# Attention scores of two heads at a time: float32r parts in the two halves of the array's rows

## The chip, the core and the metric

One NeuronCore of a Trainium2 chip runs the whole program. The metric is the device time of one execution in microseconds; 4454.7 us is the median of three runs before the change (4446.53 to 4455.5).

## What is computed

A batch of 16 sequences of 512 tokens with 256 channels passes through four attention blocks, each behind a layer norm and with a residual. All have 16 heads of 16 channels. Cut to the core:

```python
x = x + attn_a(layernorm(x))     # causal, biases on q, k, v and the output
x = x + ffn(layernorm(x))        # tokens split in two groups by a similarity with g_info
x = x + attn_b(layernorm(x))     # rotary q and k, no mask
x = x + ffn(layernorm(x))

def ffn(x):                      # REG = 5 register tokens in front
    sim = mean over heads of cos(q, g); rescaled to 0..1
    pos = sim > 0.9
    # a token attends to the registers and to the tokens of its own group;
    # a register token takes the mean of its results over both groups
```

Everything is float32, and the softmax scores have to be exact to about that.

## The kernel before, in words

**Stages.** `PLAN` names four stages, a, f, b, f, here called stage 0 to 3. A stage goes through 16 batches, a batch through 4 quads of heads (`NG`), a quad through 4 key tiles of 128 keys (`NT`). So a batch has 16 key tiles.

**Scores in bf16 parts.** A float32 q or k is split into three bf16 parts (`split3`, L329 to L338: one copy on ScalarE, one on VectorE, two subtractions on POOL), and the six products of parts that matter are laid under each other on the contraction rows (`QPARTS`, `KPARTS`): 6 x 16 = 96 rows (`ROWS`). Two rows more carry the group flags of stages f, and two the negated row maximum. The parts go to DRAM (`qd`, `kd`) and come back as two quads of heads at a time (`load_half`, L489 to L510, on the SP queue, three buffers), the flag rows straight from `fd`. One matmul over at most 100 rows gives the scores of one head, 128 x 512.

**Each score is computed twice.** `maxima` (L523) makes the tile s with queries on the partitions (L545) and VectorE takes its maxima (L547; with the causal mask in L552). At the end of a quad `put` (L577 to L588) transposes the maxima on TensorE (mt, L579, in the large score banks), copies them on ScalarE (ms, L581), writes them to DRAM (md, L583) and reads them back into two rows of q (L585); both DMAs are SP's. `products` (L594) then makes the tile t with keys on the partitions (L612), the maximum already subtracted by those rows; in stage a a second matmul adds the causal mask (L620). ScalarE takes exp (L623), and `weigh` (L627, matmul L634) multiplies four heads with the values, side by side in four groups of 32 columns. The sum of a quad is copied to O in L650.

**Fill.** All else is generators: `prep` (layer norm, projections L324 and L415), `tail` (L779: transposes L793 and L813, output projection L833), `registers` (L655) and `masked`. They are drained between scores, after each of the 16 steps of a quad, by cost (`drain`, L874). Their PSUM tiles come from `small` (two banks).

**Order.** The main loop (L919 to L967) emits a t, then advances the maxima, which stay 36 steps ahead (`AHEAD`, four steps per key tile); a `put` follows its last maximum by 8 steps (`WAIT`, L914). The value products of a key tile come one key tile later (`waiting`). Between a and f and between b and f everything is drained and `split` computes the flags. The framework then places each instruction in its engine's queue: in this order, but with others moved ahead where one would wait by its own planning. [...] Fill and scores use different banks: five of 512 columns for s and t, one for the value sums, two for `small`.

Of the kernel before, what the change touches and what calls it, by code (L numbers as in the profile page):

```python
# [40 lines left out]
P = 128  # L42
# [5 lines left out]
RW = 4 * (32 + REG)  # L48
# [6 lines left out]
AHEAD = 36  # L55
WAIT = 8
QPARTS = (0, 1, 2, 0, 1, 0)
KPARTS = (0, 0, 0, 1, 1, 2)
ROWS = 96
# [3 lines left out]
def constants():  # L63
# [7 lines left out]
    c["mask_t"] = np.ascontiguousarray(f(-BIG) * up.T)  # L71
# [4 lines left out]
    c["cos"], c["sin"] = np.repeat(cos, H, axis=0), np.repeat(sin, H, axis=0)  # L76
    c["hm"] = np.concatenate([np.tile(np.eye(H, dtype=f), (8, 1)), np.zeros((P, H), f)], axis=1)
    blk, half = np.zeros((P, H, HV), f), np.zeros((P, REG), f)
    rows = np.zeros((2, 2, RW), f)
    for h in range(H):  # L80
        p, k = 32 * (h // 4), h % 4
        for r in range(REG):
            blk[p + REG * k + r, h] = 1.0
            half[p + REG * k + r, r] = 0.5
            rows[1, :, (32 + REG) * k + r] = 1.0
    c["blk"], c["half"], c["rows"] = blk, half, rows
    clamp = np.full((P, NT, 4), -MASKED, f)
    clamp[P - 1, NT - 1] = 3.0e38
    c["clamp"] = clamp
    reg = np.zeros((P, B, NT), f)  # L90
# [7 lines left out]
def hybrid_kernel(ctx: ExitStack, tc: tile.TileContext, a: dict, out: bass.AP):  # L98
# [3 lines left out]
    def pool(name, bufs, **kw):  # L102
# [10 lines left out]
        pool("pe", 9),  # L113
# [5 lines left out]
    ps_x = pool("ps_x", 5, space=PSUM)  # L119
    ps_o = pool("ps_o", 1, space=PSUM)  # L120
    ps_s = pool("ps_s", 2, space=PSUM)
# [17 lines left out]
    qd = [dram.tile([3, C, S], BF, tag=f"qd{b}", name=f"qd{b}") for b in range(B)]  # L139
    kd = [dram.tile([3, C, S], BF, tag=f"kd{b}", name=f"kd{b}") for b in range(B)]  # L140
    vd = [dram.tile([P, NT, VW], F32, tag=f"vd{b}", name=f"vd{b}") for b in range(B)]
    xd = [dram.tile([P, NT, C], F32, tag=f"xd{b}", name=f"xd{b}") for b in range(B)]
    fd = dram.tile([4, B, S], BF, tag="fd", name="fd")
    md = [dram.tile([NT, 2, 4, P], BF, tag=f"md{i}", name=f"md{i}") for i in range(8)]
# [10 lines left out]
    ident_bf = const.tile([P, P], BF, tag="ident_bf", name="ident_bf")  # L155
    nc.vector.tensor_copy(ident_bf, ident)
# [5 lines left out]
    def load_weights(layer, project):  # L162
# [7 lines left out]
        for i in ws:  # L170
            raw = ptmp.tile([P, 2, C], F32, tag="tmp", name=f"wraw{layer}_{i}")
            nc.sync.dma_start(raw, a[f"{kind}_w"][:, :, i, :])
            if i == WQ:
                nc.vector.tensor_scalar(raw, raw, SCALE, None, ALU.mult)
            k = 0 if project else i
            nc.scalar.copy(wh[:, :, k, :], raw)
            nc.vector.tensor_tensor(wl[:, :, k, :], raw, wh[:, :, k, :], ALU.subtract)
# [9 lines left out]
    bqk = load_const("bqk", [P, 2, 2])  # L187
# [6 lines left out]
    NB = 3  # L194
    Qs, Ks = [], []
    for i in range(NB):
        q = res.tile([P, 8, S], BF, tag=f"qs{i}", name=f"qs{i}")
        k = res.tile([P, 8, S], BF, tag=f"ks{i}", name=f"ks{i}")
        Qs.append(q)
        Ks.append(k)  # L200
# [6 lines left out]
    for i in range(2):  # L207
        t = res.tile([ROWS + 2, 2, RW], BF, tag=f"rst{i}", name=f"rst{i}")
        rst.append(t)
    sim = res.tile([P, B * NT], F32, tag="sim", name="sim")  # L210

    def constant_rows():
        both = ptmp.tile([4, 2, S], BF, tag="tmp", name="zo")
        nc.vector.memset(both[:, 0], 0.0)
        nc.vector.memset(both[:, 1], 1.0)
        for q, k in zip(Qs, Ks):
            for i, t in enumerate((q, k)):
                nc.sync.dma_start(t[ROWS : ROWS + 4], both[:, i].unsqueeze(1).to_broadcast([4, 8, S]))
        for t in rst:
            nc.gpsimd.memset(t, 0.0)  # L220
# [4 lines left out]
    def early_constants():  # L225
        late["mask_s"] = to_bf("mask_s", [P, S])
        late["mask_t"] = to_bf("mask_t", [P, P])
        late["clamp"] = load_const("clamp", [P, NT, 4])
# [4 lines left out]
    def direction():  # L233
# [13 lines left out]
        )  # L247
        ps = small("gt")
        for i in range(2):
            nc.tensor.transpose(ps[:, i * P : (i + 1) * P], g2[:, i * P : (i + 1) * P], ident)  # L250
# [5 lines left out]
    def late_constants():  # L256
# [7 lines left out]
        rows = p1.tile([2, 2, RW], F32, tag="rows", name="rows")  # L264
        nc.sync.dma_start(rows, a["rows"])
        rb = p1.tile([2, 2, RW], BF, tag="rb", name="rb")
        nc.vector.tensor_copy(rb, rows)
        for t in rst:
            nc.sync.dma_start(t[ROWS : ROWS + 2], rb)
# [5 lines left out]
    def prep(layer, b, x):  # L275
# [53 lines left out]
        def split3(which, i, y):  # L329

            t = p4.tile([P, 3, S], BF, tag="parts", name=f"t{which}{n}_{i}")
            nc.scalar.copy(t[:, 0, :], y)  # L332
            sub = nc.vector if which == "k" and layer + b == 0 else nc.gpsimd
            sub.tensor_tensor(y, y, t[:, 0, :], ALU.subtract)  # L334
            nc.vector.tensor_copy(t[:, 1, :], y)  # L335
            sub.tensor_tensor(t[:, 2, :], y, t[:, 1, :], ALU.subtract)  # L336
            d = (qd if which == "q" else kd)[b]
            nc.sync.dma_start(d[:, i * P : (i + 1) * P, :].rearrange("k p q -> p k q"), t)  # L338

        def parts(which, i):  # L340
            ps = small(f"p{which}{n}_{i}")
            yield from project(ps, WQ if which == "q" else WK, i)
            y = ptmp.tile([P, S], F32, tag="tmp", name=f"y{which}{n}_{i}")
            if kind == "a":
                w = 0 if which == "q" else 1
                nc.scalar.activation(y, ps, AF.Identity, bias=bqs[:, w, i : i + 1])
            else:
                nc.scalar.copy(y, ps)
            if kind == "f" and which == "q":
                y2 = ptmp.tile([P, S], F32, tag="tmp", name=f"y2{n}_{i}")  # L350
                nc.scalar.activation(y2, ps, AF.Square)
                st["y", i] = y, y2
            else:
                split3(which, i, y)

        def similar():
# [6 lines left out]
            for i in range(2):  # L363
                split3("q", i, st["y", i][0])
# [14 lines left out]
            else:  # L379
                nc.gpsimd.tensor_tensor(nd[:, 0], nd[:, 0], nhalf, ALU.pow)  # L380
# [4 lines left out]
        def turned(which):  # L385
# [10 lines left out]
            nc.vector.tensor_tensor(b_, y[1], sin, ALU.mult)  # L396
            nc.gpsimd.tensor_tensor(a_, a_, b_, ALU.subtract)
            nc.vector.tensor_tensor(b_, y[0], sin, ALU.mult)
            nc.gpsimd.tensor_tensor(y[1], y[1], cos, ALU.mult)
            nc.gpsimd.tensor_tensor(y[1], y[1], b_, ALU.add)  # L400
            split3(which, 0, a_)
            split3(which, 1, y[1])
# [47 lines left out]
    def split(layer):  # L450
# [22 lines left out]
        fl = p1.tile([P, 4, n], BF, tag="fl", name=f"fl{layer}")  # L473
# [4 lines left out]
        pf = small(f"pf{layer}", BF)  # L478
        for k in range(4):
            nc.tensor.transpose(pf[:n, k * P : (k + 1) * P], fl[:, k, :], ident_bf)  # L480
        fs = p1.tile([n, 4, P], BF, tag="fs", name=f"fs{layer}")
        nc.vector.tensor_copy(fs.rearrange("r k p -> r (k p)"), pf[:n, : 4 * P])
        nc.sync.dma_start(fd.rearrange("k b (t p) -> (b t) k p", p=P), fs)


    halves = [(layer, b, u) for layer in range(len(PLAN)) for b in range(B) for u in range(2)]
    cleared = set()

    def load_half(i):  # L489
        layer, b, u = halves[i]  # L490
        kind = PLAN[layer]
        q, k = Qs[i % NB], Ks[i % NB]
        hs = slice(8 * u, 8 * (u + 1))
        if kind == "b" and i % NB not in cleared:
            cleared.add(i % NB)
            nc.gpsimd.memset(q[ROWS : ROWS + 2].bitcast(F32), 0.0)
        for dst, src, blocks in ((q, qd[b], QPARTS), (k, kd[b], KPARTS)):
            src = src.rearrange("k (d h) s -> (k d) h s", h=H)
            r = 0
            while r < 6:  # L500
                e = r + 1
                while e < 6 and blocks[e] == blocks[e - 1] + 1:
                    e += 1
                p0 = D * blocks[r]
                nc.sync.dma_start(dst[D * r : D * e], src[p0 : p0 + D * (e - r), hs, :])
                r = e
        if kind == "f":
            f = slice(ROWS, ROWS + 2)
            nc.sync.dma_start(q[f], fd[0:2, b, :].unsqueeze(1).to_broadcast([2, 8, S]))
            nc.sync.dma_start(k[f], fd[2:4, b, :].unsqueeze(1).to_broadcast([2, 8, S]))  # L510
# [12 lines left out]
    def maxima(i):  # L523


        layer, b, g = quads[i]
        kind = PLAN[layer]
        half = i // 2
        q, k = Qs[half % NB], Ks[half % NB]
        rows = slice(0, ROWS + 2) if kind == "f" else slice(0, ROWS)  # L530
        n = f"{layer}_{b}_{g}"
        st = {}

        def score(t, j):
            if "mx" not in st:
                st["mx"] = p2.tile([P, NT, 4], F32, tag="mx", name=f"mx{n}")
            end = (t + 1) * P if kind == "a" else S
            m = S // end
            if j % m == 0:
                spare = layer + 1 == len(PLAN) and j == 0  # L540
                name = f"s{n}_{t}_{j}"
                st["ps"] = small(name) if spare else ps_x.tile([P, S], F32, tag="x", name=name)
            h = 4 * (g % 2) + j
            ps = st["ps"][:, (j % m) * end :][:, :end]
            nc.tensor.matmul(ps, q[rows, h, t * P : (t + 1) * P], k[rows, h, :end], start=True, stop=True)  # L545
            if kind != "a":
                nc.vector.tensor_reduce(st["mx"][:, t, j : j + 1], ps, AX.X, ALU.max, negate=True)  # L547
            elif j % m == m - 1:
                for i in reversed(range(m)):
                    ps = st["ps"][:, i * end : (i + 1) * end]  # L550
                    w = p1.tile([P, S], BF, tag="scr", name=f"sc{n}_{t}_{j}")[:, :end]
                    nc.vector.tensor_tensor_reduce(  # L552
                        w,
                        ps,
                        late["mask_s"][:, S - end :],
                        1.0,
                        -3.0e38,
                        ALU.add,
# [455 lines left out]
```

## Time and profile before

| | |
|---|---|
| median of 3 runs | 4454.7 us |
| the profiled execution's own time | 4459.03 us |
| its span | 4457.3 us |
| mean granted TensorE clock | 0.972 |
| instructions | 76135 |
| exp (L623) | 3776, 594 ns on average |
| maxima (L547) | 3072, 682 ns |
| scores (L545, L612) | 8192 |
| value products (L634) | 8192 records, two for each float32 matmul |
| power on POOL (L380) | 30, 10.6 us each |
| read from and written to HBM | 291.18 and 174.19 MB |

A row of a timeline gives the start, the duration, the engine, the line, the tile written from the tiles read, and the shape. [...] A group row gives the count, the busy time, the mean, and behind the last bar the idle time of the engine ahead of these instructions with what ended it. A row of waits gives the total, the number and the longest. PEld is the load of the weights. The last O copies of the stages stand at 1224.4, 2360.0, 3436.4 and 4441.0 us, the first at 101.6, 1324.2, 2376.5 and 3522.1.

### The profile page before, as it was taken

What the parts mean: (1) busy time and instruction counts of PE and PEld (TensorE: products, weight loads), DVE (VectorE), ACT (ScalarE), POOL (GpSimd) and SP (SyncE); (2) the same over time, 40 slices, a digit from 0 to 9 for tenths busy, and PEclk for the clock granted to TensorE, in tenths of its full rate; (3) what the DMA queues carried; (4) which work ended last, traced back from release to release, by engine and by line L of the source; (5) the groups of instructions that cost most, each with busy time, mean ns of one, the idle gap of its engine ahead of it and who ended that gap; (6) DMA issues with size and microseconds to landing.
All of it is one profiled execution on the core that took longest, in us unless ns stands there. A gap on an engine that the chain in (4) does not pass through costs nothing.

```text
span 4457.3 us, 76135 instructions
## 1 busy us (share of the span) xinstructions
PE 4231.9 (95%) x26672; PEld 1995.5 (45%) x26672; DVE 3392.3 (76%) x8003; ACT 2791.5 (63%) x5480; POOL 1482.9 (33%) x1302
## 2 busy tenths in 40 slices
PE   6999899999979999999999999999999799999999
PEld 4555555555534444444444444444444233333333
DVE  6776666777668888888888777777775687887885
ACT  3555455555536767767767666666666466666666
POOL 4445455554432433433433333423424100000000
PEclk8999999999979999999999999999999799999999
DMA  6544545454424444444444443444444144333441
GB/s 176 128 128 122 134 119 141 123 144 116 119 71 101 105 110 108 104 114 103 108 115 107 106 110 101 102 107 103 104 105 113 44 89 89 83 78 83 89 89 30
DMA packets 230020, 470.56 MB, mean 106 GB/s; under 512 B 45630, under 2 KB 176004, under 8 KB 205060
## 3 DMA queue, kind: packets, MB, share of 16 engines
q1 hardware_dynamic: 229636, 465.69, 42.6%
q8 instruction: 211, 3.46, 0.3%
q14 instruction: 173, 1.42, 0.1%
HBM read 291.18 MB, written 174.19 MB: 104 GB/s over the span
## 4 chain that ended last, share of the span: by engine, by line
PE 75%; DMA 12%; DVE 4%; ACT 3%; POOL 2%; issue 2%; SPq 1%; ACTq 0%; POOLq 0%; DVEq 0%
PE po L634 19%; PE t L612 17%; PE s L545 16%; DMA md<-ms 5%; PE pj L833 4%; PE pq L324 3%; PE pv L415 3%; PE pk L324 3%; ACT e L623 3%; DMA x<-in_x 2%; PE ot L793 2%; DMA qs<-qd 2%; PE rs L675 1%; DMA qs<-md 1%; DVE mx L547 1%
## 5 line engine op out<-in xcount | busy, mean ns | idle before, releaser
L623 ACT ACTIVATE e<-t 128x512 f32<-128x512 f32 (+1 forms) x3776 | 2053.4, 594 | 865.7 <-PE t L612 588.7
L547 DVE TENSOR_REDUCE mx<-s 128x1 f32<-128x512 f32 x3072 | 1970.6, 682 | 517.0 <-PE s L545 507.2
L612 PE MATMUL t<-qs,ks 100*128 100x512 bf16 (+3 forms) x4096 | 1422.6, 364 | 61.1 <-DMA qs<-md 37.5
L545 PE MATMUL s<-ks,qs 98*128 98x512 bf16 (+4 forms) x4096 | 1404.9, 367 | 57.9 <-DMA ks<-fd 16.9
L634 PE MATMUL po<-e,v 128*32 128x512 f32 (+1 forms) x8192 | 1071.1, 569 | 7.5 <-ACT e L623 4.9
L612 PEld LDWEIGHTS <-ks 100*128 100x128 bf16 x4096 | 397.8, 98 | 779.1 <-issue 528.9
L545 PEld LDWEIGHTS <-qs 96*128 96x128 bf16 (+1 forms) x4096 | 386.0, 99 | 597.9 <-issue 383.3
L552 DVE CUSTOM_DVE_ANT_0 sc<-s,mask_s_bf 128x128 bf16<-128x128 f32 (+3 forms) x1024 | 497.7, 486 | 172.5 <-PE s L545 134.6
L634 PEld LDWEIGHTS po<-e,v 128*32 128x32 f32 x8192 | 172.2, 108 | 407.6 <-issue 290.2
L380 POOL TENSOR_TENSOR nd<-nd,nhalf 128x64 f32<-128x64 f32 x30 | 316.8, 10561 | 0.0
L290 POOL TENSOR_SCALAR st<-mv 128x4 f32<-128x4 f32 x64 | 16.0, 251 | 884.3 <-DVE mv L287 849.7
L664 POOL COPY rst<-qs 96x40 bf16<-96x40 bf16 x64 | 14.6, 229 | 859.6 <-DMA qs<-qd 336.4
L334 POOL TENSOR_TENSOR yq<-yq,tq 128x512 f32<-128x512 f32 x112 | 131.1, 1177 | 296.9 <-ACT e L623 155.7
L650 ACT COPY o<-po 128x512 f32<-128x512 f32 x256 | 150.8, 589 | 110.5 <-PE po L634 107.8
L789 POOL TENSOR_TENSOR x<-x,f_bo 128x1024 f32<-128x1024 f32 x32 | 76.0, 2376 | 404.2 <-DMA x<-xd 308.1
L620 PE MATMUL t<-mask_t_bf,ident_bf 128*128 128x128 bf16 x1024 | 203.8, 223 | 0.0
L793 PE MATMUL ot<-ident,o 128*128 128x128 f32 x1024 | 182.7, 291 | 18.1 <-DVE vst L427 12.4
L306 POOL TENSOR_SCALAR xn<-x,nm,st 128x256 f32<-128x256 f32 x256 | 142.4, 561 | 116.0 <-PE xp L310 102.7
L332 ACT CAST tk<-yk 128x512 bf16<-128x512 f32 x112 | 69.3, 619 | 173.1 <-DMA qd<-tq 170.3
L793 PEld LDWEIGHTS ot<-ident,o 128*128 128x128 f32 x1024 | 129.4, 148 | 78.0 <-DVE vst L427 15.2
L336 POOL TENSOR_TENSOR tk<-yk,tk 128x512 bf16<-128x512 f32 x110 | 128.3, 1168 | 95.5 <-DVE tk L335 89.8
L335 DVE CAST tq<-yq 128x512 bf16<-128x512 f32 x112 | 88.6, 793 | 77.3 <-POOL yq L334 76.8
(365 smaller groups left out, 5509.4 us busy)
## 6 DMA issues: line engine op xcount, KB each, us to landing
ks<-kd SPq DMA_DIRECT2D x256, 256.0 KB
qd<-tq SPq DMA_DIRECT2D x128, 384.0 KB
qs<-qd SPq DMA_DIRECT2D x128, 384.0 KB
kd<-tk SPq DMA_DIRECT2D x128, 384.0 KB
vd<-vst SPq DMA_DIRECT2D x64, 576.0 KB
v<-vd SPq DMA_DIRECT2D x64, 576.0 KB
qs<-qd SPq DMA_DIRECT2D x128, 256.0 KB
ks<-kd SPq DMA_DIRECT2D x256, 128.0 KB
```

The source lines that it names most:

```text
L324: nc.tensor.matmul(dst, ww[:, c, w, cols], xx[:, c, :], start=(k == 0 and c == 0), stop=(k == 2 and c == 1))
L380: nc.gpsimd.tensor_tensor(nd[:, 0], nd[:, 0], nhalf, ALU.pow)
L545: nc.tensor.matmul(ps, q[rows, h, t * P : (t + 1) * P], k[rows, h, :end], start=True, stop=True)
L547: nc.vector.tensor_reduce(st["mx"][:, t, j : j + 1], ps, AX.X, ALU.max, negate=True)
L552: nc.vector.tensor_tensor_reduce(w, ps, late["mask_s"][:, S - end :], 1.0, -3.0e38, ALU.add, ALU.max, st["mx"][:, t, j - m + 1 + i : j - m ...
L612: nc.tensor.matmul(ps, k[: ROWS + 4, h, t * P : (t + 1) * P], q[: ROWS + 4, h, q0:], start=True, stop=(kind != "a"),)
L620: nc.tensor.matmul(ps[:, :P], ident_bf, late["mask_t"], start=False, stop=True)
L623: st["exp", t] = nc.scalar.activation(e[:, : m * w], st["ps"][:, : m * w], AF.Exp)
L634: mm = nc.tensor.matmul(st["po"][32 * j : 32 * j + 32, q0:], v[:, t, h * HV : h * HV + 32], E.pop((t, j)), start=(t == 0), stop=(t == NT - 1),
L650: nc.scalar.copy(o, st["po"])
L793: nc.tensor.transpose(ps[:, g * P : (g + 1) * P], O[layer, b, g][:, t * P : (t + 1) * P], ident)
L833: nc.tensor.matmul(ps[:, k * C : (k + 1) * C], aa[:, k, c, :], ww[:, c, 0, :], start=(q == 0 and c == 0), stop=(q == 2 and c == 1),)
```

## The change

Q and k are split into two float32r parts, and three products of parts take 3 x 16 = 48 rows. With flag and maximum rows 52 are used of each half of the 128 rows, and two heads (even and odd) stand in the two halves. The scores of two heads are two matmuls, one in each half, into the two banks of a double tile; one reduction or one exp takes both. `load_quad` brings one quad (6 buffers) on POOL's queue, from `qd` and `kd` that are now float32 and hold the constant and flag rows as well (`constant_rows`, `split`). Maxima go back once per two quads, in two float32r parts: transposed in a `small` bank, ScalarE's copy, a subtraction on VectorE, a write on SP's queue and four reads on POOL's. Fill is drained once per key tile. PSUM is dealt anew: three double tiles for s and t, one bank for values, one for `small`. In stage b the rotation runs on POOL alone.

```diff
-RW = 4 * (32 + REG)
+RI = 96 + 2 * REG
+RW = 2 * RI
-AHEAD = 36
-WAIT = 8
-QPARTS = (0, 1, 2, 0, 1, 0)
-KPARTS = (0, 0, 0, 1, 1, 2)
-ROWS = 96
+AHEAD = 24
+WAIT = 3
+ROWS = 48
+HALF = 64
...
-        pool("pe", 9),
+        pool("pe", 5),
...
-    ps_x = pool("ps_x", 5, space=PSUM)
+    ps_x = pool("ps_x", 3, space=PSUM)
     ps_o = pool("ps_o", 1, space=PSUM)
-    ps_s = pool("ps_s", 2, space=PSUM)
+    ps_s = pool("ps_s", 1, space=PSUM)
...
-    NB = 3
+    NB = 6
...
-        q = res.tile([P, 8, S], BF, tag=f"qs{i}", name=f"qs{i}")
+        q = res.tile([P, 2, S], FR, tag=f"qs{i}", name=f"qs{i}")
...
+        def split2(which, i, y):
+            t = p4.tile([P, 2, S], FR, tag="parts", name=f"t{which}{n}_{i}")
+            nc.gpsimd.tensor_copy(t[:, 0, :], y)
+            nc.gpsimd.tensor_tensor(t[:, 1, :], y, t[:, 0, :], ALU.subtract)
+            send(which, i, t)
...
+                nc.scalar.copy(t[:, 0, :], ps)
+                nc.vector.tensor_tensor(t[:, 1, :], ps, t[:, 0, :], ALU.subtract)
+            send(which, i, t)
...
-                nc.gpsimd.tensor_tensor(nd[:, 0], nd[:, 0], nhalf, ALU.pow)
+                for t in range(NT):
+                    nc.gpsimd.tensor_tensor(nd[:, 0, t], nd[:, 0, t], nhalf[:, t], ALU.pow)
...
+    def load_quad(i):
+        layer, b, g = quads[i]
+        for t, d in ((Qs[i % NB], qd[b]), (Ks[i % NB], kd[b])):
+            nc.gpsimd.dma_start(t, d[:, :, 2 * g : 2 * g + 2, :].rearrange("e r h s -> (e r) h s"))
...
+            for e in range(2):
+                r = slice(HALF * e, HALF * e + n_rows)
+                nc.tensor.matmul(
+                    st["ps"][:, e, (p % m) * end :][:, :end],
+                    q[r, p, t * P : (t + 1) * P],
+                    k[r, p, :end],
+                    start=True,
+                    stop=True,
+                )
+            if kind != "a":
+                nc.vector.tensor_reduce(st["mx"][:, :, 2 * g + p, t], st["ps"], AX.X, ALU.max, negate=True)
...
+            def put():
+                ps = small(f"mt{n}")
+                rows = NT * 8
+                nc.tensor.transpose(ps[:rows, :P], mx.rearrange("p j t -> p (j t)"), ident)
+                ms = p2.tile([rows, 2, P], FR, tag="ms", name=f"ms{n}")
+                nc.scalar.copy(ms[:, 0, :], ps[:rows, :P])
+                nc.vector.tensor_tensor(ms[:, 1, :], ps[:rows, :P], ms[:, 0, :], ALU.subtract)
+                d = md[half % len(md)]
+                nc.sync.dma_start(d.rearrange("k e j t p -> (e j t) k p"), ms.bitcast(F32))
+                for g in range(2):
+                    for e in range(2):
+                        r = HALF * e + ROWS
+                        nc.gpsimd.dma_start(
+                            Qs[(2 * half + g) % NB][r : r + 2],
+                            d[:, e, 2 * g : 2 * g + 2].rearrange("k j t p -> k j (t p)"),
+                        )
...
+            for e in range(2):
+                nc.tensor.matmul(
+                    ps[e],
+                    k[rows[e], p, t * P : (t + 1) * P],
+                    q[rows[e], p, q0:],
+                    start=True,
+                    stop=(kind != "a"),
+                )
             if kind == "a":
-                nc.tensor.matmul(ps[:, :P], ident_bf, late["mask_t"], start=False, stop=True)
+                for o in range(2):
+                    for e in range(2):
+                        mk = late["mask_t"][HALF * e : HALF * (e + 1), o]
+                        nc.tensor.matmul(ps[e][:, :P], mk[:, 0], mk[:, 1], start=False, stop=(o == 1))
+            if p % m == m - 1:
+                e_ = pe.tile([P, 2, S], F32, tag="e", name=f"e{n}_{t}_{p}")
+                st["exp", t] = nc.scalar.activation(e_[:, :, : m * w], st["ps"][:, :, : m * w], AF.Exp)
...
-        load_through(min(end // 2 - 1, i // 2 + (2 if i else 1)))
+        load_through(min(end - 1, i + (4 if i else 3)))
...
-            for j in range(4):
-                score(t, j)
-                to = 4 * (NT * i + t) + j + 1 + AHEAD
+            for p in range(2):
+                score(t, p)
+                to = 2 * (NT * i + t) + p + 1 + AHEAD
...
-                slots = ((1 if i == 0 else NG - g) * NT - t) * 4 - j
-                drain(1.0 / max(1, slots - 3))
+                if p == 1:
+                    slots = (1 if i == 0 else NG - g) * NT - t
+                    drain(1.0 / max(1, slots - 1))
```

## The prediction, made before the changed kernel ran

> **What bounds the kernel now.** I read the page first: engine totals, slices, chain.
>
> ```profile
> PE 4231.9 (95%) x26672; PEld 1995.5 (45%) x26672; DVE 3392.3 (76%) x8003; ACT 2791.5 (63%) x5480; POOL 1482.9 (33%) x1302
> PE   6999899999979999999999999999999799999999
> PEclk8999999999979999999999999999999799999999
> PE 75%; DMA 12%; DVE 4%; ACT 3%; POOL 2%; issue 2%; SPq 1%; ACTq 0%; POOLq 0%; DVEq 0%
> ```
>
> TensorE is full everywhere except at the start and at two passages between stages, where its granted clock falls too. Whether busy is work shows only in the starts, so next comes the timeline of TensorE in the last stage:
>
> ```profile
> 3803.68 0.38 PE L545 MATMUL s<-ks,qs 98*128 98x512 bf16 x1
> 3803.89 0.38 PE L612 MATMUL t<-qs,ks 100*128 100x512 bf16 x1
> 3804.20 1.06 PE L634 MATMUL po<-e,v 128*32 128x512 f32 x8
> 3805.20 0.39 PE L545 MATMUL s<-ks,qs 98*128 98x512 bf16 x1
> 3805.43 0.38 PE L612 MATMUL t<-qs,ks 100*128 100x512 bf16 x1
> ```
>
> The column after the start is a duration, but a score begins 0.22 us after the one before. After a score the value products begin 0.31 later: 0.09 for changing from the whole array to 32 columns. A value group takes 1.06 with both changes. The float32r price and the way back from it:
>
> ```profile
> 2599.86 0.63 PE L324 MATMUL pk<-xl,whq 128*128 128x512 f32 x2
> 2600.33 0.62 PE L324 MATMUL pk<-xh,whq 128*128 128x512 f32 x2
> 2600.80 0.39 PE L545 MATMUL s<-ks,qs 96*128 96x512 bf16 x1
> ```
>
> Two float32r products take 0.47, so 0.235 each, against 0.22 in bf16. Twelve of 256 columns (pj) take 1.41 (0.12 each); four transposes 0.44 (0.11 each). Then the groups of VectorE and ScalarE, and the queue of SP:
>
> ```profile
> L623 ACT ACTIVATE e<-t 128x512 f32<-128x512 f32 (+1 forms) x3776 | 2053.4, 594 | 865.7 <-PE t L612 588.7
> L547 DVE TENSOR_REDUCE mx<-s 128x1 f32<-128x512 f32 x3072 | 1970.6, 682 | 517.0 <-PE s L545 507.2
> SPq L585 <- DMA md<-ms: 719.2, 252, 8.3
> PE t L612 <- DMA qs<-md: 37.5, 27, 4.6
> PEld L612 <- DMA qs<-md: 49.5, 35, 4.7
> ```
>
> VectorE and ScalarE wait for TensorE. The maxima go through DRAM: SP waits 2.85 us on average for the write before it may issue the read (0.62 us), which lands some 2.1 us later (chain of waits). TensorE lost only 87 us to that, because a quad's first t stands far behind its transposition mt: 9.4, 12.2, 10.6 and 13.8 us by their starts in every batch of stage 1.
>
> **TensorE's work.** Stages run a, f, b, f; a batch (four quads, 16 key tiles) takes 71.3, 65.7, 67.3 and 58.3 us, from the first and last O copies (L650) of each stage. Stage 1 checks the prices: 128 scores x 0.218 = 27.9; 16 value groups x 1.06 = 17.0; 36 transposes x 0.11, 24 pq/pk x 0.23, 48 pv/pj x 0.12 and register work give 18.6. Sum 63.5 of 65.7.
>
> After: 64 pairs. If the halves run at once, a pair costs one float32r product, 0.235: 15.0, so 12.9 less. No row here shows row halves. The nearest are the value products, four column groups whose starts lie 7 ns apart, eight records in 1.0 us. I take 0.235 and keep 0.47 (no concurrency) as the other end. [...] But bf16 loads (98 ns) of the same rows disappear in a step of 0.22 here, and the float32r step of 0.235 holds its 190 ns load; the trace decides.
>
> Mode changes rise: the order of the built program has 1094, 1020, 1056 and 966 per stage against 718, 730, 744 and 768. At 0.09 that is 2.1, 1.6, 1.8 and 1.1 us a batch. Half as many mt save 0.4; registers add 0.2 in f stages. [...] So before waits: stage 0 71.3 - 7.3 + 2.1 - 0.2 = 65.9; stage 1 54.2; stage 2 55.8; stage 3 46.3.
>
> **VectorE, ScalarE, PSUM.** The forms of L552 grow from 286 ns (128 columns) to 685 (512): 1.04 ns an element, 0.15 fixed. A 1024-wide reduction is 1.22 for two at 0.682; exp likewise 1.03 for two at 0.60 (384 columns take 493). VectorE in stage 3: 32 x 1.22 + 7.7 of other work = 46.7, above TensorE's 46.3. Only three double score slots remain for five single ones: a slot passes from t to s after the exp (0.24 + 0.2 + 1.03 + 0.1) and the second s of a key tile waits for it with po behind it. Written out for one key tile without fill, the step is 2.9 us. I take stage 3 at 50, and add 2 us a batch in stages 1 and 2, where this largely lies beside fill. Dropping the third part frees VectorE's casts and POOL's subtractions; neither bounded, so no gain. qd, kd and qs grow from 2 to 4 bytes for fewer rows: 470 MB becomes about 620 at DMA rows now 40 to 50% busy; the copies are a quad ahead, so zero, up to +50 if late.
>
> **The new wait.** What is lost is distance. AHEAD falls from 36 of four steps per key tile to 24 of two, and WAIT puts mt six steps (three key tiles) before its use; and mt now shares the only small bank (ps_s 1, ps_x before) with every fill. In the built order mt stands behind the fills' uses of it. TensorE work (by the prices above) between mt and the first t that needs it, for the two halves of a batch:
>
> - stage 0: 2.8 and 1.0 us (before, per quad, 8 to 14)
> - stage 1: 2.3 and 7.3 (9 to 13)
> - stage 2: 4.2 and 2.0 (9 to 15)
> - stage 3: 7.7 and 6.8 (10 to 12)
>
> The round trip: mt 0.3; ms on ScalarE 0.25 plus half an exp 0.5; the new subtraction on VectorE 0.3 plus half a reduction 0.6; SP issue 0.3; write 2.6; then POOL, no longer SP, issues the read: two issues before a first pair, in order behind element-wise work of 1.2 us a piece, about 2.3; landing 2.1. Sum 9.2; I use 9. No POOL-issued transfer is in this trace; ends 6.5 (POOL free, issues as short as SP's) and 12 (behind two operations and a load that waits for TensorE). Behind the waiting t in TensorE's queue stand all s, po and fill, so ScalarE and VectorE empty and stop. Loss per batch, 9 minus the distances: 14.2, 8.4, 11.8 and 3.5.
>
> **Sum per batch**: stage 0 65.9 + 14.2 = 80.1 (+8.8); stage 1 54.2 + 2 + 8.4 = 64.6 (-1.1); stage 2 55.8 + 2 + 11.8 = 69.6 (+2.3); stage 3 50 + 3.5 = 53.5 (-4.8). Together +5.2, x 16 = +83. Passages: 24 pairs ahead at VectorE's 1.22 = 29.3 for 36 x 0.68 = 24.6 in stages 1 and 3, and the flag rows take one more DRAM hop (64 issues, the first four on the path): +20. Clock: this trace halves it for 3.4 to 10 us after idle stretches of some us; about 80 new waits above 5 us at 1 us each: +80 (0 to 200). Total +183 on the profiled run (span 4457.3, its own time 4459.0); on the median 4454.7: 4638, so 4640.
>
> **Rivals.**
>
> - Faster: the same chain in 6.5 us. Losses 9.2, 4.2, 6.8 and 0 a batch save 283, less clock loss 60: 4295. For it: before, first t stood only 7.8 us behind mt in stage 0 and did not wait. Against: VectorE's step, the shared bank and POOL are new in the chain. It decides at about 7.7 us.
> - POOL late: a chain of 12 us, 128 us for each one more: 5020. For it: stage 1's POOL gets rotations and splits (25 us a batch at 1.2 to 1.3 each) and 16 issues. Against: its idle share, 67%.
> - The halves do not run side by side, or pay each load: +15 a batch on TensorE, +9 in stage 0; less what VectorE's bound and longer distances cover, about 5250. The value groups' 7 ns speak against it.
>
> **Numbers.** Round-trip case 0.46 (4640, own range 4480 to 4830); faster 0.28; late POOL 0.12; no concurrency 0.10; gain and loss cancel within 0.2% 0.04. A measurement of this kernel tells about 0.2% (9 us) from no change. Slower 0.68, same 0.04, faster 0.28. Range 4280 to 5050: most of the faster case, late POOL, not the last.
>
> **What would show it.** Right: s and t start in couples some ns apart, couples 0.24 apart; TensorE's busy share falls to about 75%; t waits for DMA qs<-md some 600 us, most in stages 0 and 2; the clock row shows 8s and 9s in mid-stage; VectorE near 70%. Wrong: couples 0.45 apart; a chain under 8 us; waits for ms or for slots in place of md; POOL full.

## The result and the profile after

The changed kernel takes 5018.97 us in the median of four runs (4998.75 to 5059.2), the kernel before 4455.1 on the same chip: a ratio of 1.128 (95% interval 1.121 to 1.135), slower by 564 us where I had said 185. The profiled execution took 4998.75 us, its span is 4997.0. First the page:

```profile
PE 4196.8 (84%) x27312; PEld 2070.2 (41%) x27312; DVE 3137.8 (63%) x5760; ACT 2477.8 (50%) x3240; POOL 1812.5 (36%) x2421
PE   4878887888778588988988888888888858999998
PEclk7888888889988689999989989999988969999999
PE 48%; ACT 9%; DVE 5%; DMA 3%; issue 2%; SPq 1%; POOL 1%; ACTq 0%; DVEq 0%; POOLq 0%
```

TensorE has lost its full row of nines: mostly 8s and 7s, but for the last stage, which is full and at full clock. No other engine has become full. In the chain TensorE falls from 75% to 48%. By stage (the windows run from the first to the last O copy of each stage):

```profile
core 0: us, PE busy (x) PEld busy (x) DVE busy (x) ACT busy (x) POOL busy (x), PEclk, DMA share, GB/s
122.00:1592.00 1470.00, 1206.18 (x8749) 693.65 (x8749) 773.84 (x2740) 526.75 (x766) 521.13 (x616) 0.87 0.47 139
1728.00:2864.00 1136.00, 1019.82 (x6354) 474.59 (x6350) 765.18 (x949) 657.69 (x845) 577.36 (x782) 0.91 0.44 132
2894.00:4017.00 1123.00, 964.75 (x5781) 453.08 (x5777) 726.29 (x907) 640.36 (x802) 437.21 (x501) 0.92 0.45 131
4148.00:4973.00 825.00, 774.25 (x5462) 320.99 (x5461) 680.79 (x769) 576.69 (x721) 177.88 (x367) 1.00 0.34 105
```

The three stages with much fill run at 0.87 to 0.92 of the clock; the one with little fill runs at 1.00, with the same pairs. All numbers "a batch" from here on are means over the last 15 batches of a stage, from the O copies; idle and half clock come from TensorE's records and from the granted clock in the same stretch.

| us a batch | stage 0 | stage 1 | stage 2 | stage 3 |
|---|---|---|---|---|
| before | 72.1 | 66.4 | 67.4 | 58.0 |
| after | 94.3 | 72.8 | 71.9 | 52.4 |
| TensorE idle, before / after | 5.2 / 17.0 | 0.3 / 7.4 | 1.0 / 10.3 | 1.7 / 3.1 |
| at half clock, before / after | 5.0 / 24.4 | 0 / 12.3 | 0 / 12.5 | 1.4 / 0 |

The 539.7 us between the two spans are: start 20.5, stage 0 346.9, passage 36.5, stage 1 99.9, passage 14.0, stage 2 62.5, passage 45.3, stage 3 -93.5, end 7.6.

The pairs do what the change says. TensorE's timeline in the last stage (start, duration; x2 is one pair):

```profile
4500.56 0.50 PE L639 MATMUL t<-qs,ks 52*128 52x512 f32 x2
4500.89 0.40 PE L566 MATMUL s<-ks,qs 52*128 52x512 f32 x2
4501.29 0.50 PE L639 MATMUL t<-qs,ks 52*128 52x512 f32 x2
4502.23 0.50 PE L566 MATMUL s<-ks,qs 52*128 52x512 f32 x2 [0.45 <-ACT e L653]
```

A duration runs on beside the next pair: 0.50 in the first row, with the second 0.33 later. In stage 3 the second matmul of a pair starts 2 to 4 ns behind the first in 774 of 932 pairs (0 to 15 in all), and the median from pair to pair is 0.23 us; the first pair after other work takes 0.34, as from the first row to the second (0.33). The mean times of the wide exp and the wide reduction are near what was worked out:

```profile
L653 ACT ACTIVATE e<-t 128x1024 f32<-128x1024 f32 (+2 forms) x1920 | 1856.2, 997 | 1004.8 <-PE t L639 658.8
L574 DVE TENSOR_REDUCE mx<-s 128x2 f32<-128x1024 f32 x1536 | 1858.8, 1220 | 583.5 <-PE s L566 522.0
```

The wait on which my sum rested is small. From the waits over the whole span:

```profile
POOL qs L611 <- DMA md<-ms: 600.4, 116, 14.2
PE t L639 <- DMA qs<-md: 69.9, 44, 10.1
PEld t L639 <- DMA qs<-md: 58.6, 52, 10.8
```

It is POOL that waits 600 us for the write. TensorE waits for the read 70 us ahead of its matmuls and 59 ahead of its weight loads; these overlap, and together they cover 91 us. What else TensorE waits for shows in stage 0 alone (122 to 1592 us). The read has the longest single row, 21 us. Far more in sum, some 200 us, are the rows of fill, where TensorE waits for an evacuation (the copy of a result out of PSUM) or for data made from one; most come 13 or 14 times, about once a batch:

```profile
PE t L639 <- DMA qs<-md: 21.4, 18, 2.9
PE pk L347 <- DVE tk L390: 20.5, 14, 2.2
...
PE pq L347 <- DVE xl L337: 16.5, 9, 2.2
PE sq L398 <- ACT y L379: 15.3, 13, 1.2
PE sf L797 <- DVE xt L801: 13.9, 26, 0.5
```

A stretch of the timeline around one mt, in stage 0, shows both (PEld left out, idle time before the instruction in brackets):

```profile
906.33 0.38 PE L828 MATMUL ot<-ident,o 128*128 128x128 f32 x2
906.75 0.44 DVE L832 TENSOR_TENSOR xt<-ot,xt 128x272 f32<-128x272 f32 x1 [0.75 <-PE ot L828]
...
907.25 0.28 PE L602 MATMUL mt<-ident,mx 128*32 128x128 f32 x1 [0.53 <-DVE xt L832]
...
907.86 0.27 DVE L605 TENSOR_TENSOR ms<-mt,ms 32x128 fp32r<-32x128 f32 x1
908.16 0.32 SPq L607 DMA_DIRECT2D md<-ms  x1
908.19 0.66 PE L828 MATMUL ot<-ident,o 128*128 128x128 f32 x4 [0.66 <-DVE ms L605]
...
909.38 0.44 PE L848 MATMUL pa<-ident,on 128*128 128x128 f32 x2 [0.53 <-DVE xt L832]
...
909.92 2.06 POOL L611 DMA_DIRECT2D qs<-md  x4 [9.47 <-DMA md<-ms]
...
911.87 0.79 PE L639 MATMUL t<-qs,ks 50*128 50x512 f32 x1 [1.31 <-DMA qs<-md]
```

ot, mt, ot, pa each go into the one `small` bank, and mt, the second ot and pa each stand 0.5 to 0.7 us until VectorE has emptied it of the one before. From mt to t it is 4.6 us here, and of these TensorE waits only the last 1.31 for the maxima: the rest goes into fill and its waits. In most batches of stage 0 only fill stands between mt and the first t, in both halves (6 sf in one, 4 ot and 4 pa in the other).

Stages 1 and 2 have other long rows. s waits for a score tile that an exp has to free (29.2 and 25.0 us), in stage 1 ot waits for ScalarE's re (23.0 us, 14 times), and in stage 2 xp, the transposition for the layer norm, waits for POOL's xn: 43.8 us, 14 times, where before it did not wait for it there.

### The profile page after: what moved, and what is told of

Same layout as the page of the kernel before. It is cut to its first block, busy times and chain, and to the rows that moved or that the text cites. A ratio compares the mean times of both kernels' runs of the same rounds, so it can differ in the third digit from the quotient of the medians.

```text
span 4997.0 us, 73802 instructions
## 1 busy us (share of the span) xinstructions
PE 4196.8 (84%) x27312; PEld 2070.2 (41%) x27312; DVE 3137.8 (63%) x5760; ACT 2477.8 (50%) x3240; POOL 1812.5 (36%) x2421
## 4 chain that ended last, share of the span: by engine, by line
PE 48%; ACT 9%; DVE 5%; DMA 3%; issue 2%; SPq 1%; POOL 1%; ACTq 0%; DVEq 0%; POOLq 0%
PE po L665 15%; PE t L639 9%; PE s L566 8%; ACT e L653 7%; PE pj L868 3%; PE pq L347 3%; PE pv L453 2%; PE pk L347 2%; PE ot L828 2%; DVE mx L574 1%; DMA md<-ms 1%; PE rs L710 1%; SPq L525 1%; PE xp L333 1%; DMA qs<-md 1%
## 5 line engine op out<-in xcount | busy, mean ns | idle before, releaser
L653 ACT ACTIVATE e<-t 128x1024 f32<-128x1024 f32 (+2 forms) x1920 | 1856.2, 997 | 1004.8 <-PE t L639 658.8
L574 DVE TENSOR_REDUCE mx<-s 128x2 f32<-128x1024 f32 x1536 | 1858.8, 1220 | 583.5 <-PE s L566 522.0
L566 PE MATMUL s<-ks,qs 52*128 52x512 f32 (+4 forms) x4096 | 950.4, 456 | 213.5 <-ACT e L653 111.8
L639 PE MATMUL t<-qs,ks 52*128 52x512 f32 (+4 forms) x4096 | 999.1, 466 | 85.3 <-DMA qs<-md 69.9
L639 PEld LDWEIGHTS t<-qs,ks 50*128 50x128 f32 (+1 forms) x4096 | 436.8, 198 | 867.9 <-issue 423.3
L534 POOL DMA_DIRECT2D qs<-qd x256 | 145.6, 569 | 1324.8 <-PE s L566 732.6
L566 PEld LDWEIGHTS s<-ks,qs 48*128 48x128 f32 (+1 forms) x4096 | 420.5, 201 | 491.6 <-ACT e L653 281.3
L611 POOL DMA_DIRECT2D qs<-md x512 | 265.9, 526 | 645.3 <-DMA md<-ms 600.4
L418 POOL TENSOR_TENSOR nd<-nd,nhalf 128x16 f32<-128x16 f32 x120 | 346.0, 2900 | 88.5 <-DVE nd L409 88.5
L650 PE MATMUL t<-mask_t_bf 64*128 64x128 bf16 x2048 | 174.9, 244 | 0.0
```

The costliest lines, as they stand in the source:

```text
L418: nc.gpsimd.tensor_tensor(nd[:, 0, t], nd[:, 0, t], nhalf[:, t], ALU.pow)
L566: nc.tensor.matmul(st["ps"][:, e, (p % m) * end :][:, :end], q[r, p, t * P : (t + 1) * P], k[r, p, :end], start=True, stop=True,)
L574: nc.vector.tensor_reduce(st["mx"][:, :, 2 * g + p, t], st["ps"], AX.X, ALU.max, negate=True)
L611: nc.gpsimd.dma_start(Qs[(2 * half + g) % NB][r : r + 2], d[:, e, 2 * g : 2 * g + 2].rearrange("k j t p -> k j (t p)"),)
L639: nc.tensor.matmul(ps[e], k[rows[e], p, t * P : (t + 1) * P], q[rows[e], p, q0:], start=True, stop=(kind != "a"),)
L650: nc.tensor.matmul(ps[e][:, :P], mk[:, 0], mk[:, 1], start=False, stop=(o == 1))
```

## Experiments

**T1**, my theory after this: with one small bank every step of fill is TensorE, then evacuation, then TensorE again, and the pauses bring the half clock. **R1**: the maxima's way is what costs, as I had predicted. **R2**: fill given out in one piece per key tile is. **R4**: the clock falls because the halves of the array are used so. The numbers by stage below are us a batch, stage 0 to 3, as in the table above.

**Two small banks, single score banks, pairs kept.** Reductions and exps take one head each again.

```diff
-    ps_x = pool("ps_x", 3, space=PSUM)
+    ps_x = pool("ps_x", 5, space=PSUM)
...
-    ps_s = pool("ps_s", 1, space=PSUM)
+    ps_s = pool("ps_s", 2, space=PSUM)
...
-                nc.vector.tensor_reduce(st["mx"][:, :, 2 * g + p, t], st["ps"], AX.X, ALU.max, negate=True)
+                for e in range(2):
+                    nc.vector.tensor_reduce(
+                        st["mx"][:, e, 2 * g + p, t : t + 1], st["ps"][e], AX.X, ALU.max, negate=True
+                    )
...
-                st["exp", t] = nc.scalar.activation(e_[:, :, : m * w], st["ps"][:, :, : m * w], AF.Exp)
+                for e in range(2):
+                    st["exp", t] = nc.scalar.activation(e_[:, e, : m * w], st["ps"][e][:, : m * w], AF.Exp)
```

> The changed kernel with its PSUM dealt as before the change: five single banks for s and t, two for small (for three double tiles and one). Pairs of heads still stand side by side in the two halves of the rows; only the reductions and the exps go back to one head each, 512 wide. T1 (TensorE stands behind the evacuation of the one small bank in every fill step, and these pauses bring the half clock): the idle time of TensorE per batch falls from 17.0, 7.4, 10.3 and 3.1 us to some 5, 2, 2 and 3, the half-clock stretches go with it, batches of about 66, 57, 59 and 53 us, in all 4000 to 4300 us. R1 (the maxima's way through DRAM, with POOL's reads, is what costs): that way is the same, so 4700 to 5000. R2 (fill given out in one piece per key tile): unchanged there too, 4700 to 5000. R4 (the clock falls because the halves of the array are used so): clock as low as in the changed kernel, 0.90.

4897.98 us, ratio 1.102 (1.098 to 1.106). T1's number is missed by far. TensorE's idle time did fall (6.1, 3.8, 2.0, 2.3 a batch) and the half clock left stages 1 and 2 (0.5 and 0.7; clock 0.99 and 1.00 over the whole stages), so R4 falls; R1 and R2 don't explain that either. In stage 0 19.6 us of half clock stay, which T1 does not explain. And the batches take 89.8, 71.0, 66.7 and 59.9. For stages 1 to 3 the waits of TensorE's weight loads say why:

```profile
PEld s L566 <- DVE mx L575: 468.1, 652, 0.8
...
PEld s L566 <- ACT e L657: 176.9, 508, 1.2
```

652 + 508 waits of s for a score bank, 1.2 us at the longest, for the most part in time in which TensorE counts as busy. A score costs 0.21 to 0.25 us on average again in stages 1 to 3 (from start to start, without idle time), as without pairs; in the changed kernel's stage 3 it is 0.17 to 0.18. A pair takes two banks at a time: five single ones are two and a half places.

**One small bank in the kernel before.**

```diff
-    ps_x = pool("ps_x", 5, space=PSUM)
+    ps_x = pool("ps_x", 6, space=PSUM)
-    ps_s = pool("ps_s", 2, space=PSUM)
+    ps_s = pool("ps_s", 1, space=PSUM)
```

> The kernel before with one small bank for two, and six score banks for five; nothing else. T1: the fill's steps now wait for each other's evacuation, TensorE's idle time rises from 5.2, 0.3, 1.0 and 1.7 us a batch by 4 to 12 in stages 0 to 2, its clock falls from 0.97 to 0.93 or less, in all 4750 to 5200 us. R1 and R2: nothing that they speak of is touched, 4455 within 50 us. If it lies between (4500 to 4750), one small bank is a cost, but only a part, and needs the coarser fill or the transposition of the maxima in it as well.

5205.1 us, ratio 1.168 (1.165 to 1.170), clock 0.906: with no pair, no float32r part in q and k, and SP's reads, about as much as T1 allowed. By stage 90.0, 78.6, 67.4 and 71.8; idle 14.6, 6.2, 2.1, 10.3; half clock 25.5, 13.7, 1.1, 10.5. Over the span TensorE's rows of fill are many and short here too, and the wait for the maxima grows with them (37.5 us before):

```profile
PE t L612 <- DMA qs<-md: 83.0, 42, 3.9
...
PE ot L793 <- DVE al L823: 30.4, 35, 1.4
```

Its two passages with a drain are 81 us longer. Two limits: stage 2 is untouched, so its +4.5 in the changed kernel needs something more; and in its last stage this kernel puts every fourth s into `small` too, so that stage's +13.8 isn't fill alone.

**Without the reads of the maxima.** The reads are left out and the rows hold a constant.

```diff
+    zo[0, 0] = -40.0
...
-                for g in range(2):
-                    for e in range(2):
-                        r = HALF * e + ROWS
-                        nc.gpsimd.dma_start(
-                            Qs[(2 * half + g) % NB][r : r + 2],
-                            d[:, e, 2 * g : 2 * g + 2].rearrange("k j t p -> k j (t p)"),
-                        )
```

> The changed kernel without the four reads on POOL's queue that bring the maxima back into the rows of q; those rows hold the constant -40 from the start. So the output is not that of the reference: the scores are not shifted by their maxima. Transposition, copy, subtraction and write stay. R1 (the round trip of the maxima, as predicted): t never waits for md and POOL loses 256 issues, so the some 560 us come back, 4500 us or less. T1: only the 128 us of waits for the read in front of t go, and some of them are covered by the next wait, 4850 to 5000 us.

5086.52 us, ratio 1.142 (1.139 to 1.146): no better than the changed kernel, and above what T1 gave as well. By stage 87.2, 84.6, 71.1, 52.3. R1 falls as the main cause: stages 2 and 3 gain 0.8 and 0.1. Stage 0 gains 7.1 us a batch, about half of what I had put there. Stage 1 loses 11.8 and is not a clean reading: with the reads gone the framework placed POOL's other work otherwise, and s waits for loads of k that POOL issues late.

```profile
PE s L567 <- DMA ks<-kd: 69.2, 13, 6.1
```

**Fill in smaller pieces.**

```diff
-    if p == 1:
-        slots = (1 if i == 0 else NG - g) * NT - t
-        drain(1.0 / max(1, slots - 1))
+    slots = ((1 if i == 0 else NG - g) * NT - t) * 2 - p
+    drain(1.0 / max(1, slots - 1))
```

> The changed kernel with its fill given out after each pair of heads, twice per key tile, for once per key tile; nothing else. R2 (the piece in which fill is given out makes the waits): smaller pieces put scores between the uses of the small bank, 4700 us or less. T1: there is still one bank, each use waits for the evacuation of the one before, a little less where a pair stands between: 4850 to 5050 us.

5058.85 us, ratio 1.135 (1.133 to 1.138), just above T1's range. R2 falls. Stage 2 gains 3.0 us a batch (68.9), stage 3 loses 6.9 (59.3).

**Larger pieces in the kernel before.** The drain after each of the four steps of a key tile now comes after the fourth alone.

> The kernel before with its fill given out once per key tile for after each of the four steps; nothing else. R2 (the coarse giving-out makes the waits): 4650 us or more. T1: with two small banks the piece hardly matters, 4440 to 4580 us.

4470.94 us, ratio 1.0044 (1.0029 to 1.0059): with two banks the piece costs some 20 us.

**Three small banks, two double tiles**, and **the same with three double tiles in stage 3.**

```diff
-    ps_x = pool("ps_x", 3, space=PSUM)
+    ps_x = pool("ps_x", 2, space=PSUM)
-    ps_s = pool("ps_s", 1, space=PSUM)
+    ps_s = pool("ps_s", 3, space=PSUM)
```

> The changed kernel with its eight banks dealt otherwise: two double tiles for s and t in place of three, three small banks in place of one. T1, after the run with single banks has shown that short waits for score banks can eat what the second small bank gives back: TensorE's idle time in front of fill (projections, transposes) goes from stages 0 to 2, and the half clock with it (24, 12 and 12 us a batch to under 8, 2 and 2); but two tiles bind the scores: stage 3, which has little fill, goes from 52.4 to 58 to 66 us a batch. Stages 0 to 2 at 80 to 88, 64 to 72, 62 to 70; in all 4550 to 4950 us. R1 (the round trip of the maxima): stages 0 to 2 as in the changed kernel, over 5000 us. R4 (the clock falls because of the halves): the clock stays near 0.90.

> As the kernel with two double tiles and three small banks in stages 0 to 2, but in stage 3 one pair of the banks serves as the third double tile, as in the changed kernel. T1: stages 0 to 2 like that kernel, stage 3 at 52 to 54 us a batch; so 70 to 200 us below it, 4450 to 4800 us; if stages 0 to 2 come out below 72, 66 and 67 it also beats the kernel before, else not. R1: no better than the changed kernel, 5000 us or more.

5109.56 us (1.148, 1.145 to 1.151) and 4852.72 (1.092, 1.087 to 1.096). Both forecasts were too low. Stage by stage the first takes 79.7, 77.6, 73.3, 69.2, the second 80.1, 75.8, 75.1, 52.4. In the first no kind of fill has over 1.2 us of idle a batch in front of it any more; s alone has 9.3, 10.5 and 13.2 in stages 1 to 3, and they wait for the reduction that frees a tile:

```profile
PEld s L566 <- DVE mx L574: 1216.7, 1077, 2.5
```

So the wait moved from one pool to the other. Only stage 0 gains on the changed kernel (14.6), and even there no dealing comes to the 72.1 of before.

**mt earlier.** WAIT is 1 for 3.

> The changed kernel with WAIT at 1 for 3: the transposition of the maxima stands one key tile earlier in TensorE's order, so that some 7 steps for 5 lie between it and the first t that needs it. Without the reads stage 0 gained 7 us a batch and stages 2 and 3 nothing. T1: so stage 0 gains 1 to 5 us a batch, the others nothing, and mt may wait a little for the last maxima: 4930 to 5050 us. R1: every stage gains 2 steps of distance, 3 to 6 us in each batch of stages 0 to 2, 4750 to 4870 us.

5165.42 us, ratio 1.161 (1.158 to 1.164): against both theories. Ahead of t TensorE waits 160 us for the read where it was 70. In TensorE's order mt did move, but with other fill and no scores behind it (in stage 0 mostly 24 pv with 2 or 4 sf where there were 6 sf, and 12 pv, half the time with 4 ot, where there were 4 ot and 4 pa). More distance in the loop was not more distance in the queue. Why the framework chose so stays open.

**Pairs in stage 3 alone.** If the banks are the matter, pairs pay only where fill is thin. So stages 0 to 2 of the kernel before, then stage 3 of the changed one:

```diff
+    deal(5, 2, 0)     # single score banks, small banks
     for i, (layer, b, g) in enumerate(quads):
+        if layer == 3:
+            break
...
+    deal(3, 1, 1)     # double tiles, small bank
+    for i in range(first_i, len(quads)):
...
+        score, weigh = products2(i)
```

> Both kernels in one: stages 0 to 2 as in the kernel before (six bf16 parts, one head at a time, five score banks, two small ones, 36 steps ahead), stage 3 as in the changed kernel (pairs of heads in the halves of the rows, three double tiles, one small bank, 24 steps ahead); the banks are dealt anew between the two, when everything is drained. T1 (pairs pay where the fill is too thin to need a second small bank): stages 0 to 2 at 72, 66 and 67 us a batch as before, stage 3 at 52 to 53 for 58.0; that is 16 x 5.6 = 90 us less, of which the passage into stage 3 takes back 15 to 45 (flag rows by way of DRAM, other tiles in place of the old): 4380 to 4430 us. R4 (using the halves of the array lowers the clock, whatever else): stage 3 at half clock in stretches, no gain. R1: stage 3 waits for the maxima's way, 58 us a batch or more, 4455 or more.

4405.43 us against 4449.81, ratio 0.9906 (0.9892 to 0.9919): 0.9% faster than the kernel before. The batches take 71.9, 66.3, 66.6 and 52.3, with no half clock in stages 1 to 3; the passage into stage 3 is 19 us longer. But the first O copy came at 122.9 us for 101.6, much as in the changed kernel (122.1). SP's queue in the timeline of the start shows writes of constant rows for the last stage:

```profile
16.46 0.64 SPq L266 DMA_DIRECT2D qe<-in_zo  x1
...
19.31 1.24 SPq L266 DMA_DIRECT2D ke<-in_zo  x2
```

All 64 stand between 16 and 114 us; they wait for nothing, and the framework had moved them to the front.

**The same, with each of these writes waiting for its own batch.**

```diff
+    tc.add_manual_dep(put.ins, after.ins.name, ...)   # after: a step of this batch in stage 2
```

> The kernel with the pairs in stage 3 alone, where the 64 writes of constant rows to DRAM, which the framework had moved to the front of SP's queue since they wait for nothing (16 to 114 us of the profile, 1 MB for each batch), now each wait for a step of their own batch in stage 2. In both kernels that have these writes the first O copy came at 122 to 123 us for 101.6. If SP's queue at the start is the cause, the first O copy comes back to 102 +- 4 us and the whole to 4375 to 4392 us. If the start is late for another reason (other tiles, loads of the pair's constants), 4400 or more.

4391.36 us against 4456.14, ratio 0.986 (0.984 to 0.988). The writes now stand between 2447 and 3443 us, and the first O copy is back at 101.5. Its page reads full and at full clock but for the passages, and lighter on TensorE than before (4231.9 us there):

```profile
PE 4103.8 (94%) x26514; PEld 1982.5 (45%) x26514; DVE 3328.7 (76%) x7367; ACT 2700.5 (62%) x4872; POOL 1553.6 (35%) x1596
PE   6999899999979999999999999999999689999998
PEclk8999999999979999999999999999999799999999
```

## Why the prediction went wrong, step by step

The sign was right; the mechanism and the size were not. The step that failed is "The new wait": "Loss per batch, 9 minus the distances". From mt to the landing of the second read it is 5.8, 8.2, 7.2 and 7.0 us in the median of the four stages, so 9 was high. The distances failed: I counted TensorE's work between mt and t and gave nothing for the waits in between. I had written that mt "shares the only small bank (ps_s 1, ps_x before) with every fill" and set no price for it. The one bank makes TensorE wait ahead of much of its fill, and in stage 0 these waits stand in the very stretch in which I let it wait for md. So TensorE waits 91 us for the read, not some 600, and taking the reads away (7.1 us a batch in stage 0, about nothing in 2 and 3) doesn't give the time back. The 87 us that the prediction reads for the kernel before has the same overlap in it: 37.5 and 49.5 cover 50 us together.

That the sum of the waits (+37.9 a round of one batch of each stage) came near the measured +29.7 is luck, since they are other waits. What was mis-sized is TensorE's work, the clock, and the start and passages.

The forecast in its own terms, summed over one batch of each stage, against what was measured. The clock term is an estimate: half of the growth of TensorE's busy time at half clock (40.5 us for 5.0). The work is what waits and clock leave of the +27.5 a round; idle time for score slots stands with the work in the forecast and with the waits in what was measured.

| us | forecast | measured |
|---|---|---|
| TensorE's work | -32.7 (slots +7.7) | -20.0 |
| its waits | +37.9 | +29.7 |
| clock | 80 / 16 = +5 | +17.8 |
| the stages together | 16 x 10.2 = 163 | 416 (27.5 a round; the first batch of a stage loses less) |
| start, passages, end | +20 | +124 |

- **Pairs.** From pair to pair 0.235 was right (0.23 in stages 1 to 3), and the 0.47 kept as the other end was not: that step holds a pair's two loads, 183 ns each in the median. No run shows the 0.45 named as a sign against it, nor a pair that pays for its loads. But few pairs stand beside pairs. In stage 3 one behind value products or fill takes 0.34, one ahead of fill 0.33, one between the two 0.43 (medians), where a bf16 score took 0.22 to 0.23 and only ahead of work on 32 columns 0.31. So 64 pairs take 22.5 us, 0.35 each, where single scores took 30.3. That is 7.8 us saved, where 12.9 less 1.1 for mode changes was forecast; in stages 1 and 2 it is 5.5 and 7.5.
- **Narrow pairs.** The sum takes 7.3 us off stage 0 for them, a term that no run shows: s and t together take 19.0 us a batch before and 18.3 after, some of it at half clock, and 17.4 with three small banks in the second dealing. The causal mask, for which the sum has no term, takes 6.3 us a batch for 5.0.
- **VectorE, ScalarE, slots.** 1.22 and 1.03 were right. Idle time in front of s, 2.9 us a batch in stage 3, shows the slots' price. That stage 3 came out at 52.4 for 53.5 is luck in part: 3.5 us were to be waits for md, of which 0.1 came, and the pairs saved 4 us less. That three double tiles suffice there was right; that nothing else pays for them was not.
- **Clock.** +80 was for 80 waits above 5 us. About 280 came (16 x 17.8, an estimate), mostly with chains of short waits: 43 us of half clock more in a round of four batches.
- **Passages and start.** +20 was for 24 pairs and the flag rows; the drained fill goes through one bank there (+96 together, +82 with one small bank in the kernel before), and SP's queue at the start was not thought of (+20.5; that its writes of constant rows cost this was shown in the kernel with pairs in stage 3 alone).
- **Rivals.** Late POOL came to the right time (5020 for 5019) by a wrong cause: t waits for the read only 91 us in all. What POOL does hold up is xp in stage 2, 2.9 us a batch. No concurrency is refuted (2 to 4 ns from half to half, 0.23 us from pair to pair). The faster case would have been decided by a way under 7.7 us; in three stages of four the way was shorter than that, and the kernel was slower all the same.
- **What would show it wrong**: "waits for ms or for slots in place of md" is what came; ms itself appears among these waits (ot and sf behind it).

What remains for theory: T1 in its first form fell with the single banks. What the dealings fit, though it is argued and not shown, is that the eight banks that every dealing shares out bound it: a pair takes two at once, so score tiles, the value bank and fill can't all be doubled, and each dealing tried (6+1+1, 5+1+2, 4+1+3) moves the wait. Shown are the cost of one small bank (in the kernel before), the move of the waits, and the gain where fill is thin. Open are why stage 0 stays near 80 even with three small banks and keeps its half clock with two, and how stage 2's share divides between the bank, mt in it, POOL's xn and the pieces. Not tried in the kernel with pairs throughout: mt in a bank of its own, and the reads on SP's queue.

## What to carry to other kernels

A change that makes two things run at once may need two of every buffer they pass through (here a pair took two banks, and fill was left with one for two; that alone took the kernel before to 5205.1 us from 4455.8): price the buffers it takes away from other work first, by asking of each instruction in the queue whose evacuation it will wait for. Distance between two instructions is their work plus the waits in between (4.6 us from mt to t in the stretch above, of which 1.31 are the wait for the maxima), and several waits in one stretch weren't added here: without the reads stage 0 gained 7.1 us a batch of the 14.2 put there. And a change that loses as a whole may win in the one stage where what it takes away isn't needed (4391.36 us for 4456.14 with the pairs in stage 3 alone).

## What the hardware showed that I hadn't expected

- The two matmuls of a pair, 52 rows each in the two halves of the array, start 2 to 4 ns apart in 774 of 932 pairs of stage 3, and from pair to pair it is what one float32r product takes (0.23 us). Next to other work a pair took about 0.1 us more, next to fill as well (0.34 behind it, 0.33 ahead of it), where a single score beside fill took 0.22.
- Half clock came behind short waits too. The granted clock is 1.0 or 0.5 in both traces, and each stretch of half clock lasts 3.41 us or a multiple of it, up to 23.9 us before and 61.4 after (but for the last of each trace). In the changed kernel TensorE was busy 0.38, on average, in the 3.41 us just ahead of a half-clock stretch, 0.77 in the 3.41 us before these and 0.90 in those before that; in the kernel before 0.33, 0.90 and 0.95. Of such pieces at full clock, those in which it was busy less than 0.43 were all followed by half clock (45, and 18 in the kernel before), of those between 0.43 and 0.5 it was 20 of 40 (7 of 9), and of those over 0.5 it was 14 of 1066 (5 of 1200). The stretch around mt above is such a case: half clock from 910.7 to 920.9 us, behind waits of 0.31 to 0.78 us, and four ot take 0.66 us at 908.19 and 1.11 at 913.34. In the kernel with single banks 14 of 44 stretches follow a piece in which TensorE was busy over 0.7; their cause is open. The changed kernel has 79 stretches, 1044 us in all, for 30 and 254 us before.
- POOL issues a read of the maxima in 0.53 us (L611) and a load in 0.57 (L534); SP's write of the maxima takes 0.32.
